# A two-layer graph network on one core: the first graph's transposes by halves, the last graph's last head by itself

## The chip, the cores and the metric

The kernel runs on one core of one Trainium2 chip. A core has a matrix engine (TensorE, in the profile PE, its weight loads PEld), a vector engine (VectorE, DVE), a scalar engine (ScalarE, ACT), GpSimd (POOL) and SyncE (SP), which here issues nearly all DMAs. Each engine works through its own list of instructions in order; semaphores hold an instruction back until its inputs are there. The metric is the time of one execution on the device, in microseconds (us); of several executions the median is given.

## The reference

Sixteen graphs, each with 1024 nodes of 256 features (`x`) and an adjacency matrix `adj` (int32; in these data 0 or 1, symmetric, ones on the diagonal). Two layers, each followed by a residual sum and a layer norm over the features (no gain, no offset):

```python
# layer 0: gate every edge by a sigmoid of a bilinear score, then sum over neighbours
e0    = leaky(einsum('bid,bjd->bij', x * a0[:, 0], x))        # slope 0.2
alpha = sigmoid(where(adj == 1, e0, -big))    # e1, e2, e3 for adj == 2, 3, 4
x     = layernorm(x + einsum('bij,bjd->bid', alpha, x) + bias)
# layer 1: graph attention, 4 heads of 64
Wh    = (x @ W).reshape(B, N, 4, 64)
e     = leaky_relu(e_src[:, :, None] + e_dst[:, None, :], 0.2) # Wh with a_src, a_dst
alpha = softmax(where(adj > 0, e, -1e9), axis=2)
x     = layernorm(x + elu(einsum('bijh,bjhf->bihf', alpha, Wh)).reshape(B, N, 256))
```

## The kernel before

All sixteen graphs go through a fast path that holds for adjacency of 0 and 1 and for scores of moderate size. While it runs it gathers three things that tell whether that held: sums of each adjacency matrix and its transpose (`sums`), the span of the attention scores (`span`), and the largest reciprocal of a softmax denominator (`zinv`). At the end they become one flag; it is loaded into a register of every engine (L1339), and a branch (L1342) leads to a general path that is not taken with these data.

**One graph.** Nodes stand in eight blocks of 128 (index `ib` or `jb`), in two halves of four. The function `stages` (from L197) makes a dictionary of Python generators, one for each kind of step; each `yield` ends one step.

- Loading: `xload` (L256, in two halves for the first graph, whole for the others), `aload` (L264, eight DMAs of 512 KB into two buffers), `cast` (L273, adjacency to bf16 on ACT, with its sum). The transposed adjacency comes from `turn`: in the first graph by PE (L283), in all others by a transposing DMA on SP's queue (L288). `mask` (L295, ACT) makes the 0/1 mask from it.
- Layer 0: `xt` transposes x on PE (L308), four blocks into one PSUM tile: for each of two feature blocks `c` and each half of the nodes; `xtc` copies the result to SBUF (L318; in the first graph on DVE, else on ACT). `xta` multiplies by a0 (L330 on DVE in the first graph, L332 on ACT in the others); `a_sb` holds a0 to a3, and a0 is loaded in `make_constants` (L65) by SP, after the two halves of x and two blocks of adjacency. `score` (L344, PE) needs both feature blocks of 512 nodes at a time. Then `leak` (L356, ACT), `leaky` (L364, DVE), `sigmoid` (L370, ACT), the transposes of the lower triangle (`below`, L383, PE, tile `pg`), masking (`lower` L389, `upper` L400, `self_loop` L407, DVE), `agg` (L415, PE), `residual` (L447), layer norm (`moments` L432, `gathered` L438, `spread` L456 and L457 on POOL, `shift` L465, `norm` L475 on DVE or L477 on ACT).
- Layer 1: transposes (`yt` L486), projection by W with the score vectors `wa` appended (`project` L505, `wh`), scores of sources (`sources` L523, `rows` L529, through DRAM at L541 and back as a broadcast, `sload` L636, tile `sbc`: one load for each half and head). The exponential of the leaky sum is split into products of factors, so that the softmax is a sum over edges with a positive score (`pos`, L646 on DVE, a comparison with the mask) and over all edges (`total`, L701 on PE, from `allm`, L693 on ACT). `acc` (L658, PE) sums `pos` against the factors `gm`, which are kept in a high and a low part (L621 ACT, L628 DVE). `acc_low` (L673, ACT) and `acc_sum` (L681, DVE) bring both parts together in `u`, for each half, head and pair of blocks.
- The end of a graph: `weigh` (L758, then a multiplication by `rho`), `divide` (L768, L771, L773, a multiplication by the reciprocal), `elu` (L793, ACT), `join` (L785, L787), layer norm, and the store (`leave`, L802 on SP; two stores for the second half of the last graph), which also updates `zinv` (L804). The multiplications (`times`) are one DVE operation for both blocks and all heads (L751); in the last two graphs they are eight small ACT operations instead (L746).

**Order.** `issue` (L1142) sorts all steps of all graphs by a time, and calls them in that order; the framework keeps the order as it is. The times only set the order. Three tables hold them: FIRST for the first graph, LAST for the last, TIMES for the fourteen between, which repeat with a period of 112. So the work of neighbouring graphs is interleaved: layer 0 of a graph beside layer 1 of the one before. Two `xload`s and two `aload`s precede all of it, then the constants. The checks that make the flag (L1316 to L1337) come after the whole planned list, outside it, and the framework's own scheduler places them: some DVE operations of them run ahead of the last `acc`, the rest after the last norm.

PSUM: four banks with the tag `pt` serve every transposed block, score, `agg`, `tot` and `pw`; two larger tiles serve `acc`. Four SBUF buffers with the tag `sbc` serve `vecs` (the score vectors), `wa`, the products and the broadcast rows.

Of the kernel before, what the change touches and what calls it, by code (L numbers as in the profile page):

```python
# [47 lines left out]
def make_constants(nc, k, const, work):  # L48
    D = k.D
    k.ident = const.tile([P, P], F32, name="ident")  # L50
    make_identity(nc, k.ident)
    k.ident16 = const.tile([P, P], BF16, name="ident16")
    make_identity(nc, k.ident16)
    k.mhalf = const.tile([P, 1], F32, name="mhalf")
    nc.gpsimd.memset(k.mhalf, -0.5)
    k.ones_r = const.tile([P, P], F32R, name="ones_r")
    ones = work.tile([P, P], F32, tag="ones", name="ones")
    nc.gpsimd.memset(ones, 1.0)
    nc.scalar.copy(k.ones_r, ones)
    k.ones = k.ones_r.bitcast(F32)  # L60
    k.a_sb = const.tile([P, k.DC, NK], F32, name="a_sb")
    k.w_aug = const.tile([P, k.DC, k.WD], F32, name="w_aug")
    k.bias_bc = const.tile([P, D], F32, name="bias_bc")
    a0 = k.inputs[0][0]
    nc.sync.dma_start(out=k.a_sb[:, :, 0:1], in_=a0.rearrange("(c p) o -> p c o", p=P))  # L65
# [131 lines left out]
def stages(nc, k, pl, b, xg, adjg, outg, sums, span, zinv):  # L197
# [104 lines left out]

    def xt():
        for c in range(DC):
            for half in range(NH):
                pt = t["xt", c, half] = quads("pt")
                for q in range(NQ):
                    nc.tensor.transpose(  # L308
                        pt[:, q, :], t["xb"][:, half * NQ + q, c * P : (c + 1) * P], k.ident
                    )  # L310
                yield

    def xtc():
        t["xT"] = pl.big.tile([P, DC, N], F32, tag="xT", name="xT")
        for c in range(DC):
            for half in range(NH):
                copy = nc.vector.tensor_copy if first else nc.scalar.copy
                copy(  # L318
                    t["xT"][:, c, half * HALF : (half + 1) * HALF],
                    t["xt", c, half].rearrange("p q n -> p (q n)"),  # L320
                )
                yield
# [391 lines left out]
    def parts(half, pair):  # L714

        u = t["u", half, pair]
        return u[..., 0:F], u[..., F : 2 * F], u[..., 2 * F], u[..., 2 * F + 1]

    def second(half, pair):

        return t["u", half, pair][..., F : 2 * F + 1]

# [18 lines left out]
    def times(val, by):  # L741

        if late:
            for q in range(2):
                for h in range(H):
# [7 lines left out]
    def weigh():  # L753
        for half, pair in PAIRS:
            ib = half * NQ + 2 * pair
            u2 = second(half, pair)
            if half:
                nc.vector.tensor_tensor(u2, t["ts", pair][..., 0 : F + 1], u2, ALU.subtract)  # L758
                yield
            times(u2, t["rho"][:, ib : ib + 2])  # L760
            yield

    def divide():
        t["rz"] = small("rzs", NB, H)
        for half, pair in PAIRS:
            ib = half * NQ + 2 * pair
            o, u2, z2, z1 = parts(half, pair)
            nc.vector.tensor_tensor(o, o, u2, ALU.add)  # L768
            yield
            rz = t["rz"][:, ib : ib + 2]  # L770
# [8 lines left out]
    def join():  # L779
        for half, pair in PAIRS:  # L780
            o, ex, _, _ = parts(half, pair)
            yp = t["y", half][:, 2 * pair : 2 * pair + 2, :].rearrange(
                "p q (h f) -> p q h f", h=H
            )
            nc.vector.scalar_tensor_tensor(o, o, 0.0, yp, ALU.max, ALU.add)  # L785
            yield
            nc.vector.scalar_tensor_tensor(yp, ex, 1.0, o, ALU.min, ALU.add)  # L787
            yield

    def elu():  # L790
        for half, pair in PAIRS:
            o, ex, _, _ = parts(half, pair)
            nc.scalar.activation(ex, o, AF.Exp)  # L793
            yield

    def leave():
        for half in range(NH):
# [5 lines left out]
            if half == NH - 1:  # L803
                nc.vector.tensor_tensor(zinv, zinv, t["rz"], ALU.max)  # L804
            yield

# [11 lines left out]
        weigh=weigh(), divide=divide(), elu=elu(), join=join(),  # L818
        moments1=moments("1"), gathered1=gathered("1"),
        spread1=spread("1"), shift1=shift("1"), norm1=norm("1"), leave=leave(),  # L820
    )

# [104 lines left out]
    "leave": [206.44, 240.93],  # L927
}
FIRST = {
    "aload": [-145.70, -145.40, -144.40, -143.60, -141.20, -140.10],  # L930
    "cast": [-146.10, -145.60, -144.60, -143.90, -142.60, -142.00, -140.90, -139.50],
    "turn": [-145.90, -145.10, -144.50, -143.20, -142.30, -141.30, -140.30, -139.30],
    "mask": [-145.30, -144.90, -143.80, -142.80, -141.70, -141.10, -139.40, -139.10],
    "setup": [-142.90, -140.70, -138.30],
    "xt": [-147.20, -147.10, -147.00, -146.80],
    "xtc": [-146.90, -146.70, -146.60, -146.40],
    "xta": [-146.50, -145.80, -144.20, -142.20, -141.80, -139.90, -139.60, -137.00],
    "score": [
        -146.20, -145.50, -144.80, -144.70, -143.40, -143.10, -142.10, -141.50, -140.40,
        -138.90, -138.60, -136.60,  # L940
    ],
    "leak": [
        -145.20, -144.30, -144.10, -144.00, -143.00, -142.70, -141.60, -141.40, -139.70,
        -138.50, -137.70, -136.40,
    ],
    "leaky": [
        -145.00, -143.70, -143.50, -143.30, -142.40, -141.90, -141.00, -140.60, -139.20,
        -137.90, -137.30, -135.60,
    ],
    "sigmoid": [-142.50, -140.80, -138.20, -137.10, -136.10, -135.00, -133.50, -132.80],  # L950
    "below": [
        -140.50, -140.20, -138.80, -138.00, -137.50, -136.80, -135.70, -135.20, -134.30,
        -132.70,
    ],
    "lower": [
        -140.00, -139.80, -138.40, -136.70, -136.00, -135.90, -134.90, -134.70, -133.40,
        -131.90,
    ],
    "upper": [-139.00, -137.60, -136.50, -135.10, -134.20, -133.00, -132.30, -131.80],
    "self_loop": [-138.70, -137.40, -135.50, -134.60, -133.80, -132.50, -131.60, -131.20],  # L960
    "agg": [
        -138.10, -137.80, -137.20, -136.20, -135.30, -134.80, -134.50, -133.90, -133.60,
        -133.20, -132.60, -132.40, -132.10, -131.40, -131.30, -130.60,
    ],
    "residual": [-136.90, -134.40, -133.70, -133.30, -133.10, -132.00, -130.90, -130.20],
    "moments0": [-135.80, -134.10, -132.90, -132.20, -131.10, -130.70, -130.40, -130.10],
    "gathered0": [-135.40, -134.00, -131.70, -131.50, -130.50, -130.30, -96.07, 17.17],
    "spread0": [-131.00, 20.28],
    "shift0": [-130.80, 24.26],
    "norm0": [6.67, 11.00, 11.41, 12.51, 25.36, 25.99, 26.71, 27.01],  # L970
    "yt": [17.15, 19.47, 29.04, 29.13],
    "ytc": [19.36, 19.69, 29.17, 29.53],
    "project": [20.27, 22.38, 25.24, 26.22, 32.78, 40.85, 41.12, 41.80],
    "wh": [25.15, 27.94, 28.22, 36.80, 41.06, 42.84, 42.85, 44.25],
    "sources": [43.57, 44.67],
    "rows": [44.50, 47.17],
    "keep_rows": [46.30, 54.62],
    "top_dve": [46.04, 47.34, 49.10, 49.48, 50.03],
    "top_pe": [46.11, 49.26],
    "exps": [51.13],  # L980
    "product": [51.24, 51.61, 51.65, 55.99, 64.09, 71.97, 73.66, 74.28],
    "high": [54.44, 56.34, 58.73, 61.00, 69.95, 72.79, 74.04, 74.66],
    "low": [54.68, 57.50, 65.30, 66.50, 71.75, 77.68, 77.72, 77.72],
    "sload": [50.22, 76.32, 79.88, 84.60, 99.79, 115.99, 126.87, 141.84],
    "pos": [
        56.38, 56.65, 59.61, 60.83, 61.90, 62.47, 66.98, 72.25, 78.79, 79.58, 80.30,
        81.29, 81.91, 83.89, 85.64, 86.24, 94.25, 94.83, 97.97, 99.15, 100.99, 101.36,
        101.95, 101.97, 105.63, 106.23, 106.73, 107.47, 108.82, 109.31, 109.42, 109.44,
        111.05, 111.90, 112.37, 114.78, 114.79, 114.81, 115.82, 117.22, 117.23, 120.53,
        122.14, 122.30, 123.00, 123.69, 124.94, 127.40, 128.22, 130.84, 132.75, 133.15,  # L990
        134.26, 137.15, 140.15, 141.06, 143.44, 144.05, 145.63, 146.94, 153.65, 154.27,
        155.46, 159.89,
    ],
    "acc": [
        61.10, 61.65, 61.72, 63.59, 69.81, 72.90, 74.47, 75.10, 81.40, 83.30, 83.92,
        84.50, 84.62, 86.15, 88.72, 89.34, 98.53, 98.69, 100.90, 100.97, 102.11, 102.79,
        105.80, 106.18, 108.03, 108.18, 108.25, 109.02, 109.72, 109.72, 110.35, 110.44,
        113.56, 114.38, 116.31, 117.04, 117.43, 119.10, 119.20, 119.89, 122.26, 122.73,
        122.79, 124.03, 124.41, 124.82, 125.15, 127.73, 134.85, 139.77, 140.29, 142.76,
        143.64, 145.00, 145.14, 146.56, 153.78, 155.85, 158.96, 159.35, 164.01, 166.21,  # L1000
        166.25, 166.99,
    ],
    "acc_low": [
        76.14, 76.54, 89.55, 94.31, 106.18, 107.05, 110.80, 113.01, 119.96, 120.50,
        133.26, 133.40, 149.44, 150.74, 167.23, 167.69,
    ],
    "acc_sum": [
        78.38, 79.46, 93.10, 94.97, 106.56, 107.30, 111.03, 113.02, 120.66, 120.80,
        133.29, 134.06, 151.18, 151.58, 167.52, 167.84,
    ],  # L1010
    "all_edges": [
        -136.30, 12.13, 78.67, 81.11, 84.67, 85.86, 89.41, 101.01, 104.36, 105.17, 108.79,
# [375 lines left out]
```

## Time and profile before

| what | us |
|---|---|
| three runs | 1746.99, 1749.58, 1750.99 |
| median | 1749.58 |
| profiled execution, own time | 1748.92 |
| its span | 1747.1 |
| first score matmul starts | 9.62 |
| last `acc` ends, about | 1724.5 |
| last `bn_aggr` ends | 1737.64 |
| last norm ends | 1740.39 |
| flag made | 1741.66 |

The span runs from the first to the last instruction that the profiler shows; the execution's own time is 1.8 us longer. The page of the profile gives busy shares of each engine, the span in 40 slices (a digit is tenths of busy time), the chain of work that ended last, groups of instructions by line, and DMAs. A timeline line gives start, duration, engine, line, operation, output <- inputs, shapes, count of like instructions in a row, and in brackets how long the engine had been idle and what released it. DVEq, SPq and the like are the engines' sequencers.

### The profile page before, as it was taken

Reading aid. Unit: us, or ns where it says so; the run is one execution under the profiler, and the core shown is the slowest. Engines: PE = TensorE matmul, PEld = TensorE weight load, DVE = VectorE, ACT = ScalarE, POOL = GpSimd, SP = SyncE. Lnnn points to the kernel's source line nnn. Section 1 sums busy time; section 2 is a strip of 40 time slices with the busy share of each in tenths; the row PEclk is TensorE's granted clock in tenths of the full one; section 3 lists DMA queues with packets and bytes.
Section 4 is the critical chain, followed back from the end, with each engine's and each line's share of the span. In section 5 each row is a group of like instructions: output and inputs, shape, how many; then the busy total and the mean of one; then the engine's idle time right before and its main releaser. Section 6 shows DMA issues by size and latency. Waiting matters only on the chain.

```text
span 1747.1 us, 29629 instructions
## 1 busy us (share of the span) xinstructions
PE 1695.6 (97%) x10579; PEld 1494.8 (86%) x10579; DVE 1639.0 (94%) x3640; ACT 1237.6 (71%) x2770; POOL 107.1 (6%) x138
## 2 busy tenths in 40 slices
PE   7999999999999999999999999999999999999884
PEld 4789898998979889898998989889898998979883
DVE  4498999999999999999999999999999999999997
ACT  6673967759587685967759586685957769585675
POOL 0001000010000101000010000101000010000100
PEclk9999999999999999999999999999999999999987
DMA  5452343434334343343434334343342435331020
GB/s 184 109 127 75 93 109 88 109 91 129 90 90 101 109 119 91 98 98 91 109 93 135 81 98 108 99 115 91 97 110 78 109 74 139 79 74 49 26 67 26
DMA packets 249274, 168.60 MB, mean 97 GB/s; under 512 B 133280, under 2 KB 232736, under 8 KB 249120
## 3 DMA queue, kind: packets, MB, share of 16 engines
q1 hardware_dynamic: 249120, 166.63, 36.3%
q8 instruction: 86, 1.41, 0.3%
q14 instruction: 68, 0.56, 0.1%
HBM read 118.10 MB, written 17.04 MB: 77 GB/s over the span
## 4 chain that ended last, share of the span: by engine, by line
PE 83%; issue 7%; DVE 4%; ACT 3%; DMA 1%; POOL 0%; SPq 0%; POOLq 0%; ACTq 0%; DVEq 0%
PE agg L415 24%; PE acc L658 24%; PE tot L701 13%; PE e L344 11%; PE pw L505 6%; PE pg L383 2%; DVE pos L646 1%; PE pt L308 1%; PE pt L486 1%; DMA sbc<-sdram 1%; DMA aT<-a 0%; ACT mT L295 0%; ACT a L273 0%; DVE gm L628 0%; DVE gate L364 0%
## 5 line engine op out<-in xcount | busy, mean ns | idle before, releaser
L646 DVE SCALAR_TENSOR_TENSOR pos<-sbc,nd,mT 128x512 fp32r<-128x512 f32 x1024 | 732.0, 738 | 7.6 <-DMA sbc<-sdram 4.5
L658 PE MATMUL acc<-gm,pos 128*128 128x260 f32 x4096 | 613.3, 293 | 6.5 <-DVE u L681 2.8
L658 PEld LDWEIGHTS acc<-gm,pos 128*128 128x128 f32 x4096 | 538.7, 190 | 19.5 <-issue 3.8
L415 PE MATMUL agg<-xb,gate 128*128 128x256 f32 x2048 | 463.3, 379 | 0.0
L415 PEld LDWEIGHTS agg<-xb,gate 128*128 128x128 f32 x2048 | 380.0, 190 | 46.9 <-DVE gate L407 0.6
L701 PE MATMUL tot<-gm,allm 128*128 128x264 f32 x2048 | 328.4, 297 | 7.1 <-ACT gm L621 5.0
L701 PEld LDWEIGHTS tot<-gm,allm 128*128 128x128 f32 x2048 | 281.1, 190 | 11.7 <-ACT gm L621 5.2
L344 PE MATMUL e<-xT,xTa 128*128 128x512 f32 (+3 forms) x768 | 265.6, 490 | 3.1 <-ACT xTa L332 1.6
L344 PEld LDWEIGHTS e<-xT,xTa 128*128 128x128 f32 x768 | 135.3, 191 | 106.9 <-issue 53.4
L673 ACT COPY low<-acc 128x260 f32<-128x260 f32 x256 | 89.9, 377 | 190.3 <-PE acc L658 190.3
L693 ACT CAST allm<-mT 128x512 fp32r<-128x512 uint8 x256 | 157.5, 616 | 27.9 <-PE tot L701 26.6
L477 ACT ACTIVATE y<-y,shift,rstd 128x256 f32<-128x256 f32 x254 | 136.8, 591 | 41.8 <-DVE shift L465 41.8
L273 ACT ACTIVATE a<-a 128x1024 bf16<-128x1024 int32 x128 | 135.6, 1060 | 41.0 <-DMA aT<-a 19.3
L295 ACT ACTIVATE mT<-aT 128x1024 uint8<-128x1024 bf16 x120 | 127.2, 1060 | 6.4 <-DMA aT<-a 6.3
L456 POOL TENSOR_SCALAR std<-mv 128x4 f32<-128x4 f32 x64 | 27.0, 421 | 1626.0 <-DVE mv L438 1426.5
L364 DVE TENSOR_TENSOR gate<-e,gate 128x512 f32<-128x512 f32 x192 | 104.2, 550 | 21.3 <-ACT gate L356 21.2
L505 PE MATMUL pw<-w_aug,yT 128*128 128x264 f32 x512 | 122.2, 387 | 0.7 <-ACT yT L495 0.6
L681 DVE TENSOR_TENSOR u<-acc,low 128x260 f32<-128x260 f32 x256 | 102.1, 419 | 16.6 <-ACT low L673 16.6
L432 DVE BATCH_NORM_STATS2 st<-y 128x6 f32<-128x256 f32 x256 | 105.8, 415 | 1.2
L505 PEld LDWEIGHTS pw<-w_aug,yT 128*128 128x128 f32 x512 | 93.4, 190 | 15.6 <-ACT yT L495 1.7
L356 ACT ACTIVATE gate<-e 128x512 f32<-128x512 f32 x192 | 90.0, 486 | 14.6 <-PE e L344 14.5
L400 DVE TENSOR_TENSOR gate<-gate,mT 128x1024 f32<-128x1024 f32 (+7 forms) x128 | 95.8, 748 | 4.5 <-PE pg L383 2.4
(97 smaller groups left out, 1775.9 us busy)
## 6 DMA issues: line engine op xcount, KB each, us to landing
a<-in_adj_dram SPq DMA_DIRECT2D x128, 512.0 KB, 4.7
sbc<-sdram SPq DMA_DIRECT2D x128, 256.0 KB, 4.6
out_dram<-y SPq DMA_DIRECT2D x31, 512.0 KB, 3.5
xb<-in_x_dram SPq DMA_DIRECT2D x15, 1024.0 KB, 5.2
aT<-a SPq DMA_TRANSPOSE x120, 3.1
xb<-in_x_dram SPq DMA_DIRECT2D x2, 512.0 KB, 4.2
sdram<-srow SPq DMA_DIRECT2D x32, 8.0 KB, 1.4
out_dram<-y SPq DMA_DIRECT2D x2, 256.0 KB, 2.3
```

The source lines that it names most:

```text
L273: nc.scalar.activation(t["a16", ib], t["a32", ib], AF.Copy, accum_out=sums[:, 0, at : at + 1])
L295: nc.scalar.activation(t["mT"][:, :, ib * P : (ib + 1) * P], t["aT", ib], AF.Square, accum_out=sums[:, 1, at : at + 1],)
L344: nc.tensor.matmul(e[:, 0:n], lhsT=t["xTa", jb][:, c, :], rhs=t["xT"][:, c, at : at + n], start=(c == 0), stop=(c == DC - 1),)
L364: nc.vector.tensor_tensor(ge, t["e", jb, at][:, 0:n], ge, ALU.max)
L415: nc.tensor.matmul(agg[:, 0:D], lhsT=t["gate"][:, jb, ib * P : (ib + 1) * P], rhs=t["xb"][:, jb, :], start=(jb == 0), stop=(jb == NB - 1),)
L432: nc.vector.bn_stats(st, t["y", half][:, q, :])
L477: nc.scalar.activation(y, y, AF.Identity, bias=shift, scale=rstd)
L505: nc.tensor.matmul(pw[:, 0:WD], lhsT=t["yT"][:, c, jb * P : (jb + 1) * P], rhs=k.w_aug[:, c, :], start=(c == 0), stop=(c == DC - 1),)
L646: nc.vector.scalar_tensor_tensor(p_, t["sbc", half, h], t["nd"][:, jb, h : h + 1], t["mT"][:, jb, half * HALF : (half + 1) * HALF], ALU.is ...
L658: nc.tensor.matmul(t["acc", half, h, q // 2][:, q % 2, 0 : 2 * E], lhsT=t["pos", half, h, jb][:, q * P : (q + 1) * P], rhs=pl.gm[:, h, jb] ...
L693: nc.scalar.copy(m_, t["mT"][:, j0 : j0 + 4, ib * P : (ib + 1) * P])
L701: nc.tensor.matmul(tot[:, 0 : H * F1], lhsT=t["allm", ib, jb // 4 * 4][:, jb % 4, :], rhs=pl.gm[:, :, jb, l, F:E], start=(jb == 0 and l == 0),
```

## The change

1. `a_sb` is allocated, and a0's DMA issued, ahead of the loads of x and adjacency; the DMA is ScalarE's instead of SP's.
2. In the first graph the transposes of x go by halves: both feature blocks of the first half, then both of the second. Of their copies, those of feature block 0 stay on DVE, those of feature block 1 go to ACT.
3. In the last graph's second half, heads 0 to 2 go through `weigh`, `divide`, `elu` and `join` without head 3, which has generators of its own: `weigh_end`, `divide_end`, `elu_end`, `join_end`. Its multiplications are on DVE instead of ACT. The joins of heads 0 to 2 are split by blocks (two instructions instead of one each). In other graphs the new generators only yield.
4. The checks become a generator, `verdict`, and take places in the planned order; the flag is now made ahead of the last norm. Every graph's update of `zinv` moves from `leave` to `verdict`.
5. FIRST and LAST have new times throughout. TIMES keeps all its values and gains those of the new generators.

In the instruction lists of both programs, PE's middle (items 861 to 7994 of 9869 compiled ones) and ACT's 1783 middle instructions stand in the same order; DVE's differ there only in the place of `zinv`. On SP, `vecs` and W are issued after adjacency block 3 of the first graph instead of block 5, and in the last graph the loads of `sbc` stand between single transposes (transpose, `aload`, `sbc`, transpose, `sbc`, transpose, `sbc`), where before two transposes stood ahead of two of them.

```diff
-    k.a_sb = const.tile([P, k.DC, NK], F32, name="a_sb")
-    a0 = k.inputs[0][0]
-    nc.sync.dma_start(out=k.a_sb[:, :, 0:1], in_=a0.rearrange("(c p) o -> p c o", p=P))
...
+        k.a_sb = const.tile([P, k.DC, NK], F32, name="a_sb")
+        nc.scalar.dma_start(out=k.a_sb[:, :, 0:1], in_=a0.rearrange("(c p) o -> p c o", p=P))
         for name in ("xload", "aload", "aload"):
             next(graphs[0][name])
...
+    PARTS = [(c, half) for c in range(DC) for half in range(NH)]
+    if first:
+        PARTS.sort(key=lambda part: part[1])
     def xt():
+        for c, half in PARTS:
...
     def xtc():
+        for c, half in PARTS:
+            copy = nc.vector.tensor_copy if first and c == 0 else nc.scalar.copy
...
+    def heads(half):
+        return slice(0, H - 1 if last and half else H)
...
     def weigh():
         for half, pair in PAIRS:
+            ib, hs = half * NQ + 2 * pair, heads(half)
+            u2 = second(half, pair)[:, :, hs]
             if half:
+                ts = t["ts", pair][:, :, hs, 0 : F + 1]
+                nc.vector.tensor_tensor(u2, ts, u2, ALU.subtract)
                 yield
+            times(u2, t["rho"][:, ib : ib + 2, hs])
...
     def join():
+            rows = (0, 1) if last and half else (slice(0, 2),)
+            for q in rows:
+                nc.vector.scalar_tensor_tensor(o[:, q], o[:, q], 0.0, yp[:, q], ALU.max, ALU.add)
...
+    END = [(H - 1, pair) for pair in range(NQ // 2)]
+    def divide_end():
+        for h, pair in END:
...
+            nc.vector.tensor_tensor(z2, z2, rho, ALU.mult)
+            for q in range(2):
+                nc.vector.scalar_tensor_tensor(
+                    o[:, q], u2[:, q], rho[:, q : q + 1], o[:, q], ALU.mult, ALU.add
+                )
+            yield
+            nc.vector.scalar_tensor_tensor(rz, z1, Z_MIN, z2, ALU.max, ALU.add)
+            yield
+            nc.vector.reciprocal(rz, rz)
+            yield
+            for q in range(2):
+                nc.vector.tensor_scalar(o[:, q], o[:, q], rz[:, q : q + 1], None, ALU.mult)
+            yield
...
     def leave():
-            if half == NH - 1:
-                nc.vector.tensor_tensor(zinv, zinv, t["rz"], ALU.max)
...
+    def verdict():
+        if last:
...
+            nc.vector.tensor_reduce(more, sums, AX.X, ALU.add)
+            nc.vector.tensor_tensor(more[:, 0:1], more[:, 1:2], more[:, 0:1], ALU.subtract)
+            nc.vector.tensor_scalar(span[:, 1], span[:, 1], -1.0, None, ALU.mult)
+            nc.vector.tensor_reduce(
+                worst[:, 1:2], span.rearrange("p s b h -> p (s b h)"), AX.X, ALU.max
+            )
+        yield
...
+        nc.vector.tensor_tensor(zinv, zinv, t["rz"], ALU.max)
+        yield
...
+            nc.vector.tensor_scalar(k.flag, good, 0.0, None, ALU.is_equal)
+        yield
```

## The prediction

> **What bounds the kernel now.** I read the page first: busy shares, slices, the chain that ended last.
>
> ```profile
> PE 1695.6 (97%) x10579; PEld 1494.8 (86%) x10579; DVE 1639.0 (94%) x3640; ACT 1237.6 (71%) x2770; POOL 107.1 (6%) x138
> PE   7999999999999999999999999999999999999884
> DVE  4498999999999999999999999999999999999997
> PE 83%; issue 7%; DVE 4%; ACT 3%; DMA 1%; POOL 0%; SPq 0%; POOLq 0%; ACTq 0%; DVEq 0%
> ```
>
> PE is full from slice 2 to slice 37; only the first slice and the last three (43.7 us each) have room. DVE, at 9 in between, is a near second. The change alters the order of the first graph, the last graph and their neighbours; the order of the middle is the same. So I read the ends by windows (columns: length, then busy time and count of PE, PEld, DVE, ACT, POOL, then clock, DMA share, GB/s).
>
> ```profile
> 0.00:10.00 10.00, 4.29 (x17) 3.55 (x18) 3.10 (x8) 2.62 (x4) 1.26 (x10) 1.00 0.66 216
> 10.00:20.00 10.00, 10.00 (x39) 5.03 (x39) 2.22 (x7) 5.69 (x12) 0.00 (x0) 1.00 0.29 100
> 20.00:30.00 10.00, 7.31 (x47) 4.32 (x45) 3.16 (x9) 9.97 (x18) 0.00 (x0) 1.00 0.66 213
> 30.00:40.00 10.00, 8.18 (x46) 5.41 (x45) 8.92 (x21) 8.97 (x18) 0.00 (x0) 1.00 0.82 273
> 1640.00:1660.00 20.00, 15.63 (x100) 13.93 (x99) 18.13 (x48) 14.44 (x47) 1.30 (x3) 0.91 0.06 16
> 1700.00:1724.50 24.50, 21.15 (x147) 19.55 (x145) 23.02 (x45) 11.26 (x41) 0.00 (x0) 0.93 0.00 1
> 1724.50:1737.70 13.20, 0.14 (x2) 0.00 (x0) 11.41 (x32) 12.16 (x41) 1.60 (x2) 0.63 0.00 0
> ```
>
> Until 10 us the kernel waits for data, then PE is the slow one, from 20 to 30 ACT (9.97 of 10), and from about 40 PE. From 1640 on DVE leads (18.13 of 20, 23.02 of 24.5), and after the last `acc`, at 1724.5, DVE and ACT hand work to and fro. Lastly the timeline of the head, and of the two places where the end waits.
>
> ```profile
> 4.41 1.09 PE L308 MATMUL pt<-ident,xb 128*128 128x128 f32 x4 [4.41 <-DMA xb<-in_x_dram]
> 6.22 2.82 PE L308 MATMUL pt<-ident,xb 128*128 128x128 f32 x12 [0.72 <-DMA xb<-in_x_dram]
> 9.19 0.48 DVE L330 TENSOR_SCALAR xTa<-xT,a_sb 128x128 f32<-128x128 f32 x2 [0.27 <-DMA a_sb<-in_L_gnn_a_dram]
> 9.62 3.75 PE L344 MATMUL e<-xT,xTa 128*128 128x512 f32 x4 [0.58 <-DVE xTa L330]
> 14.31 1.06 ACT L273 ACTIVATE a<-a 128x1024 bf16<-128x1024 int32 x1 [5.36 <-PE pa L283]
> ```
>
> ```profile
> 1556.95 11.35 SPq L288 DMA_TRANSPOSE aT<-a  x2
> 1573.24 0.75 DVE L646 SCALAR_TENSOR_TENSOR pos<-sbc,nd,mT 128x512 fp32r<-128x512 f32 x1 [2.05 <-DMA sbc<-sdram]
> ```
>
> ```profile
> 1739.30 1.09 ACT L477 ACTIVATE y<-y,shift,rstd 128x256 f32<-128x256 f32 x2 [2.16 <-DVE shift L465]
> 1741.52 0.14 DVE L1337 TENSOR_SCALAR flag<-good 1x1 int32<-1x1 f32 x1
> ```
>
> The first score matmul, at 9.62, waits for `xTa`, and that for a0 (issued 2.81, landed 6.3 later). In the tail the flag, done at 1741.66, is the last thing before a fixed 5.44 us of register loads and branches.
>
> **Head.** Before, the transposes go c0h0, c0h1 (waits for the second half of x), c1h0, c1h1; the first score needs c0h0 and c1h0. After, both first-half ones come first: four at the old pace, 4.41 to 5.50, four more to about 6.4, then the second half to 8.2. The copy of c1h0 goes to ACT: 0.56 (a 128x512 copy at L318 later on) from about 6.5. DVE copies c0h1 at 7.3 to 8.0, as the planned order has it before `xTa`, then `xTa` takes 0.48 from 8.03, and the first `e` starts at about 8.55 instead of 9.62: **1.07 us earlier**. This needs a0 by 8.0; issued at about 0.7 and at the 3.6 to 4.0 that the later loads into a_sb took (6.3 at most), it lands between 4.3 and 7.0. SP, relieved of 0.43 of issue, gains nothing: its next load waits for a buffer. `vecs` and W are issued after adjacency load 3 instead of 5; `wa` (eight DVE ops, 3.2 us) moves from 30.8 to about 24, where DVE has 3.16 of 10 busy. Were that cover gone, `xTa` behind it would cost up to 3.2.
>
> On ACT two copies (1.1) now stand before cast 0, which moves from 7.61 to about 8.85. That is hidden: its transposes follow the first `e`, at about 12. Cast 1 goes from 14.31 to 13.15, and the ACT-bound stretch follows 0.9 to 1.0 earlier in my replay (each instruction started when its inputs and engine are free, with durations from rows). By 38 us, 0.65 of `pg` work on PE is done that was not done before. From there PE is full, so the lead stays: **-1.2**. Bounds: +1.0 (a0's small pieces hold up x by as much as the 6.3 landing exceeds 3.6, less the gain) and -3.0 (PE at its later pace from the start: the four `e` took 3.75 against 1.98 at 20.26, so -1.8 more). I take the replay.
>
> The pace first: the first four `e` took 3.75 and eight turns 1.06; later the same took 1.98 and 0.61, although the clock column says 1.00 in all three windows. [...]
>
> The a0 row (6.3 us behind 2 MB of x and adjacency, against 3.6 to 4.0) says place matters. [...]
>
> **Last graph up to the last `acc`.** The 2.05 wait of DVE at 1573 (and 1.05 of PE behind it) exists because SP issued two transposes, which held its queue 11.35, ahead of `sbc`. In the new order each load of `sbc` stands behind a single one. Gain 1.05 to 2.05 if none of them waits long. Six small check operations (0.9) leave the stretch before 1724.5, where DVE leads: up to -0.9. Against it: the tables are new for the whole graph, so waits move. PE waits for `src` on ACT 2.6 and for `gm` on DVE 1.7 around 1655; in the new order the `src` of the second half comes behind 28 more `acc`, which hides some of that, while aggregation is spread later. Nearest rows for what a reordered wait is worth: 0.95 to 2.6 either way. I take **-1.5**, with -3.5 and +2 as ends.
>
> **After the last `acc`.** The last head by itself adds 20 DVE operations (subtract, four of divide's with two by rows, join; both pairs). Neighbouring rows have 0.17 (8 wide) to 0.28 (128 wide); at 0.2: +4.0. The other heads' four wide operations per pair (2.77 together) shrink to three quarters: -1.4. Joins by rows add four instructions at 0.14 (what 0.28 for 128 and 0.69 for 512 columns leave at zero columns): +0.6. Checks ahead of the norm: +0.9. Sum +4.1 of DVE work. Against that stand DVE's idle 1.8 in this window, a good 1.5 that can run before the last `acc`, since heads 0 to 2 no longer wait for head 3, and eight fewer small ACT operations of 0.25. So the last `bn_aggr` moves from 1737.6 to 1738.4, the norm's end from 1740.4 to 1741.1, and SP has issued the last store at 1741.6. The flag, ready by 1737.5, no longer adds its 1.27 us behind the norm (1740.39 to 1741.66). Those cancel: **-0.1**; ends -1.5 (the branches of the engines that wait early overlap) and +3.0 (none of the 4.1 hidden, less 1.27).
>
> **Sum.** -1.2 -1.5 -0.1 = -2.8 from the profiled execution's 1748.92: **1746.1**. That execution is 0.66 below the median of 1749.58, so against the median it is -3.5, or 0.2%: exactly where a measurement of this kernel begins to tell a difference from none.
>
> **Rivals.**
> A: PE gets its later pace during the transposes (-1.8), and the tail gives what the flag cost (-1.2): 1743.1. [...] Against it: ACT is full from 20 to 30, so an earlier PE must also find its adjacency rows loaded.
> B: the gains are hidden: a0 or the loads of adjacency still set the head, and waits in the last graph only move. Tail and head cancel: about 1748.6. For it: adjacency load 2 goes out when cast 0 frees its buffer at about 9.9 and takes 4.7 to land, so cast 2 can't come before 14.6, and DVE is over 90% busy in the last 100 us.
> C, slower: SP's queue at the start of the last graph. Three loads of `sbc` now each stand behind one transpose, which waits for its cast on ACT. A load feeds eight `pos` (8 x 0.74 = 5.9) and takes 4.6 to land, so from about 1.3 us of holding on each wait counts. At the 2.05 of the one wait in the trace, three cost 6.15, and the -1.5 doesn't come: 1748.92 - 1.2 - 0.1 + 6.15 = 1753.8. For it: two transposes held the queue 11.35. Against it: ACT is not full there.
>
> **How the numbers follow.** Forecast 0.45 (1744 to 1748; half of it below the bound of 1746.1), A 0.22, B 0.20, C 0.13. Faster by over 0.2%: 0.23 + 0.22 = 0.45; within: 0.22 + 0.20 = 0.42; slower: 0.13. The range is 1741 to 1752: it takes in A with its head at -3, B, and the ends of the last graph and the tail taken singly (+2, +3), and leaves out C.
>
> **What would show it.** Head: first `e` at 8.5, cast 1 at 13.2, PE full by 39 with the first graph's last `agg` 1.2 earlier. A0 landing after 8 or an `xTa` waiting for `a_sb` would refute it; so would `e` x4 near 2 us (A). Last graph: no DVE wait for `sbc` over 1 us; if there are three, it is C. Tail: last `acc` about 2.7 earlier than 1724.5, the span's end 22.5 after it, the flag before the last norm, DVE nearly gapless in between. Most likely wrong: the reordered last graph, whose replay is the loosest.

## The result and the profile after

Over 15 runs each the kernel before has a median of 1749.29 us (1746.8 to 1753.2) and the changed one 1744.86 (1744.0 to 1748.0). The medians are 4.4 us apart. The ratio of all runs is 0.9977, with a 95% interval of 0.9970 to 0.9983: 0.23% or 4.0 us faster. (Here and below the ratio lies near that of the means, so it can differ a little from the quotient of the medians.) The forecast was 1746.1 in a range of 1741 to 1752. The profiled execution took 1745.48, its span is 1743.5, against 1747.1 before.

The page of the changed kernel, in the lines that answer to those of before (busy times, slices of PE and DVE):

```profile
PE 1693.9 (97%) x10579; PEld 1494.5 (86%) x10579; DVE 1638.4 (94%) x3662; ACT 1240.4 (71%) x2768; POOL 106.5 (6%) x138
PE   7999999999999999999999999999999999999884
DVE  5498999999999999999999999999999999999997
```

The slices tell nothing at this size, and the chain of this page holds only the last norm, so that it says nothing on the middle. Windows of the changed kernel (length, then busy time and count of PE, PEld, DVE, ACT, POOL, then clock, DMA share, GB/s):

```profile
0.00:10.00 10.00, 3.73 (x17) 3.39 (x17) 2.01 (x7) 2.43 (x4) 1.26 (x10) 1.00 0.64 210
10.00:20.00 10.00, 9.91 (x43) 5.11 (x44) 3.50 (x10) 8.53 (x18) 0.00 (x0) 1.00 0.61 184
20.00:30.00 10.00, 7.31 (x45) 4.20 (x44) 5.97 (x15) 9.97 (x18) 0.00 (x0) 1.00 0.53 182
30.00:40.00 10.00, 8.90 (x56) 6.41 (x55) 7.46 (x17) 7.79 (x17) 0.00 (x0) 1.00 0.69 227
1721.00:1735.20 14.20, 1.02 (x4) 0.58 (x3) 13.76 (x69) 10.37 (x35) 1.42 (x2) 0.62 0.00 0
```

In the first 10 us PE does less than before (3.73 against 4.29), from 10 to 20 us ACT does half as much again (8.53 against 5.69), and after the last `acc` DVE is nearly gapless: 69 operations, 13.76 of 14.2. The timeline of the changed head shows what happened there:

```profile
6.05 3.65 PE L309 MATMUL pt<-ident,xb 128*128 128x128 f32 x16 [6.05 <-DMA xb<-in_x_dram]
9.49 0.87 DVE L330 TENSOR_SCALAR xTa<-xT,a_sb 128x128 f32<-128x128 f32 x4
9.91 2.38 PE L344 MATMUL e<-xT,xTa 128*128 128x512 f32 x4 [0.22 <-DVE xTa L330]
12.13 0.61 PE L280 MATMUL pa<-ident,a 128*128 128x128 bf16 x8
12.83 1.06 ACT L270 ACTIVATE a<-a 128x1024 bf16<-128x1024 int32 x1 [1.47 <-issue]
```

x comes 1.64 later than before (6.05 against 4.41), so the first score starts 0.29 **later**, at 9.91. But the sixteen transposes now run without a gap, the four scores take 2.38 instead of 3.75 and the eight turns 0.61 instead of 1.06, and cast 1 starts at 12.83 instead of 14.31. The last steps of the changed kernel:

```profile
1734.13 0.14 DVE L908 TENSOR_SCALAR flag<-good 1x1 int32<-1x1 f32 x1
1735.31 3.20 SPq L864 DMA_DIRECT2D out_dram<-y  x3
1736.82 1.09 ACT L477 ACTIVATE y<-y,shift,rstd 128x256 f32<-128x256 f32 x2 [1.54 <-DVE shift L465]
```

The flag is ready 3.6 ahead of the end of the last norm (1737.91); the span ends 5.6 after that norm (6.7 before).

**Where the time went.** To compare executions I cut each span at three events that all kernels have: the start of the 17th residual of layer 0 (the first of the third graph), that of the 120th (the last of the fifteenth graph), and the end of the last `acc`. "Full pace" is the instant at which the trace's clock record begins; ahead of it matmuls took about twice as long (the first four scores 3.75 ahead of it in before, 1.95 behind it in before_again; eight turns 1.06 and 0.61). All times in us. Four kernels without a median here were run once, for the profile.

| kernel | full pace | to 17th | to 120th | to last acc | to end | span | median |
|---|---|---|---|---|---|---|---|
| before | 14.47 | 235.52 | 1295.31 | 193.81 | 22.41 | 1747.05 | 1749.29 |
| before_again | 8.29 | 233.34 | 1296.07 | 193.52 | 22.84 | 1745.76 | |
| after | 10.78 | 232.97 | 1296.06 | 192.02 | 22.46 | 1743.52 | 1744.86 |
| head_only | 9.96 | 232.22 | 1297.24 | 193.93 | 22.66 | 1746.05 | 1748.53 |
| last_only | 14.14 | 235.79 | 1297.88 | 191.26 | 22.36 | 1747.29 | 1747.81 |
| a0_old | 13.30 | 233.97 | 1297.61 | 191.87 | 22.56 | 1746.02 | 1746.49 |
| a0_mid | 9.53 | 231.45 | 1297.09 | 191.53 | 22.38 | 1742.45 | 1744.84 |
| sbc_swap | 13.78 | 235.57 | 1296.35 | 191.77 | 22.44 | 1746.13 | |
| swap_timed | 9.37 | 234.26 | 1296.47 | 192.06 | 22.72 | 1745.52 | 1748.22 |
| tail_joined | 10.95 | 233.15 | 1297.29 | 191.46 | 22.88 | 1744.77 | |
| verdict_late | 9.21 | 233.96 | 1296.56 | 192.15 | 23.47 | 1746.14 | |
| before_warm | 4.79 | 233.49 | 1297.45 | 193.87 | 22.55 | 1747.36 | 1749.28 |
| mid_warm | 9.28 | 231.36 | 1296.20 | 191.83 | 22.38 | 1741.77 | 1744.91 |

Between the two profiles of the result: head -2.55, middle +0.75, last graph -1.79, tail +0.05; together -3.5. (swap_warm's profiled execution, 5 above its own median, is told of with its run; it is left out of the ranges of the stretches below.)

### The profile page after: what moved, and what is told of

Same layout as the page of the kernel before. It is cut to its first block, busy times and chain, and to the rows that moved or that the text cites. A ratio compares the mean times of both kernels' runs of the same rounds, so it can differ in the third digit from the quotient of the medians.

```text
span 1743.5 us, 29658 instructions
## 1 busy us (share of the span) xinstructions
PE 1693.9 (97%) x10579; PEld 1494.5 (86%) x10579; DVE 1638.4 (94%) x3662; ACT 1240.4 (71%) x2768; POOL 106.5 (6%) x138
## 5 line engine op out<-in xcount | busy, mean ns | idle before, releaser
L364 DVE TENSOR_TENSOR gate<-e,gate 128x512 f32<-128x512 f32 x192 | 104.3, 550 | 14.5 <-ACT gate L356 14.4
```

The source lines that it names most:

```text
L364: nc.vector.tensor_tensor(ge, t["e", jb, at][:, 0:n], ge, ALU.max)
```

## The experiments

**Head alone and last graph alone.** head_only is the kernel before with the first diff below and the changed FIRST; last_only is the changed kernel with those taken back.

```diff
-    nc.sync.dma_start(out=k.a_sb[:, :, 0:1], ...)          # behind the first loads
+        nc.scalar.dma_start(out=k.a_sb[:, :, 0:1], ...)    # ahead of them
-        for c in range(DC):
-            for half in range(NH):
+        for c, half in PARTS:                              # by halves; copies of c = 1 on ACT
```

> The kernel before with the head of the change alone: a0 first through ScalarE's queue, transposes and copies by halves, the first graph's new times; last graph and checks as before. My theory: the head is worth about half of the 4.4 us, as the lead in the trace of the changed kernel is 2.7 when the orders of both kernels meet again (270 us), and 1.7 later on: 1746.6 to 1747.6, last acc to end as before (22.6). It should show x landing near 5.9 again and not 4.3, since a0's small pieces travel beside it. Rival: the head is worth nothing by itself, because the lead is used up by the steady middle (1749), and all of the gain is the last graph's.

Measured: 1748.53, ratio 0.9990 (0.9981 to 0.9998). By the median that is 0.8 below before (1749.32 beside it), less than expected and nearer to the rival's 1749; by the ratio it is 1.7, as expected. The first stretch took 232.22, the last two 193.93 and 22.66. x landed at 5.66.

> The changed kernel with the head of before (a0 on SyncE's queue behind the first loads, transposes in the old order, four copies on VectorE, the first graph's old times); the last graph with its separate head, new times and planned checks is kept. My theory: 1.7 to 2.2 less than before (1747.1 to 1747.6), all of it ahead of the last acc, none behind it: last acc to end 22.4 to 22.7. x lands at 4.3 again and the first score starts near 9.6. Rival: the separate head and the planned checks shorten the tail by over 1, and then last acc to end is under 21.6.

Measured: 1747.81, ratio 0.9991 (0.9982 to 1.0000). That is just above what I expected. The gain of its last graph is ahead of the last `acc` (191.26 against 193.81), none behind it (22.36). The rival of a shorter tail falls. Each part shows its own stretch shortened and the other as before, so the parts don't hang together. The two medians add up to 2.3 below before, not 4.4; the two ratios add up to 0.19% of the 0.23%. With 1.5 of uncertainty each neither is a contradiction, but the stretches are the better measure.

**a0's place.** a0_old puts its load on SyncE's queue again, behind x and two blocks of adjacency; a0_mid on the same queue between them:

```diff
-        nc.scalar.dma_start(out=k.a_sb[:, :, 0:1], in_=a0.rearrange("(c p) o -> p c o", p=P))
         for name in ("xload", "aload", "aload"):
             next(graphs[0][name])
+            if name == "xload":      # a0_mid; in a0_old after the loop
+                nc.sync.dma_start(out=k.a_sb[:, :, 0:1], in_=...)
```

> The changed kernel, with a0 again on SyncE's queue behind the two halves of x and two blocks of adjacency; all else changed. My theory: x lands at 4.3 instead of 5.9, since nothing small travels beside it, and a0 at about 9, so that the first score starts at about 9.6 to 9.9, as in the changed kernel: within 0.7 of its 1744.9. Rival: a0's place is what the head gains by; then it loses about 1.5 and stands at 1746.4 or above.

Measured: 1746.49, ratio 0.9980 (0.9971 to 0.9989). By the medians it is 1.6 above the changed kernel, which is the rival's figure; by the ratios (0.9980 against 0.9977) only 0.5, which is mine. The intervals overlap, so the times don't decide between the two. x landed at 4.49, but `xTa` waited for a0 until 9.34, PE had a gap of 1.60 ahead of the first score (9.88), and full pace came at 13.30.

> The changed kernel, with a0 on SyncE's queue between the two halves of x and the adjacency. My theory: the first half of x lands at 4.3, its second half by about 1 later than 6.2 at most, a0 by 7, so the first score starts at about 8.5 and the head gains up to 1.3 on the changed kernel: 1743.6 to 1744.9. Rival: x at 5.9 in the changed kernel is chance and not a0's doing; then x lands between 4.3 and 5.9 here too, and the time is the changed kernel's.

Measured: 1744.84, ratio 0.9972 (0.9961 to 0.9983), the changed kernel's time. Its head is nevertheless what was expected: x landed at 4.54 (4.57 in mid_warm), as in all kernels with a0 behind x (4.27 to 4.86), while all four profiles with a0 first had it at 5.64 to 5.92. The two groups don't overlap, so x's later landing was no chance.

```profile
4.67 3.65 PE L309 MATMUL pt<-ident,xb 128*128 128x128 f32 x16 [4.67 <-DMA xb<-in_x_dram]
8.54 2.45 PE L344 MATMUL e<-xT,xTa 128*128 128x512 f32 x4 [0.21 <-DVE xTa L330]
11.52 1.06 ACT L270 ACTIVATE a<-a 128x1024 bf16<-128x1024 int32 x1 [1.53 <-PE pa L280]
```

Score and cast 1 come 1.3 to 1.4 earlier than in the changed kernel, and the first stretch is 1.5 shorter (231.45 against 232.97). The medians don't show that 1.5, and the ratios (0.9972 against 0.9977) only 0.9 of it: it is near what such a comparison can tell, and the middle in the table differs by up to 2.6 between executions.

**A second look at before, and one swapped pair.** sbc_swap changes a single number in LAST of the kernel before, so that SP issues transpose, `sbc`, transpose, `sbc`:

```diff
-    "turn": [..., -41.19, -35.31, -25.39],
+    "turn": [..., -41.19, -32.70, -25.39],
```

> The kernel before, unchanged, for a second profile. In the first profile the stretch from the 17th residual of layer 0 (235.5) to the 120th (1530.8) took 1295.3; in five kernels with the same order there it took 1296.1 to 1297.9. My theory: that is chance, not the change, so a second look gives 1296 to 1298 here, with 235.3 to 236.0 ahead of it, 193.6 to 194.1 from there to the last acc, and 22.4 to 22.7 behind that. Rival: something in the change makes the middle longer; then it is 1295.3 again, within 0.3.

Measured: the middle took 1296.07, as the theory had it, and 193.52 and 22.84 after it. The surprise is the head: 233.34 instead of 235.52, with the same instructions. PE's timeline of the second profile of before:

```profile
4.81 1.09 PE L308 MATMUL pt<-ident,xb 128*128 128x128 f32 x4 [4.81 <-DMA xb<-in_x_dram]
6.19 2.53 PE L308 MATMUL pt<-ident,xb 128*128 128x128 f32 x12 [0.29 <-DMA xb<-in_x_dram]
9.61 1.95 PE L344 MATMUL e<-xT,xTa 128*128 128x512 f32 x4 [0.89 <-DVE xTa L330]
11.40 0.61 PE L283 MATMUL pa<-ident,a 128*128 128x128 bf16 x8
```

The first score starts at the same 9.61, but takes 1.95 instead of 3.75: full pace came at 8.29 instead of 14.47. The four scores are 1.80 shorter for it and the eight turns behind them 0.45 (0.61 instead of 1.06), together the 2.2 by which the first stretch differs.

> The kernel before with one number changed: in the last graph's times the seventh transpose goes behind the load of the row sbc that it stood ahead of, so that SyncE issues transpose, sbc, transpose, sbc instead of two transposes and two sbc. My theory: the wait of 2.05 for sbc at the 1573rd us on VectorE goes, and with it 1.05 on TensorE; from the 120th residual to the last acc 191.8 to 192.9 instead of 193.8 (the changed kernel has 192.0, and 191.3 to 191.9 in its variants), so the swap alone gives at least half of what the last graph gained. Rival: the wait only moves to another step, and the stretch stays at 193.5 to 194; then the gain is the other new times'.

Measured: 191.77, all that the last graph's change gives (191.3 to 192.2 in the kernels with it, 193.5 to 193.9 without). The time was saved where the wait had been. Windows from 1560 to 1600, first of before, then of sbc_swap:

```profile
1560.00:1600.00 40.00, 38.72 (x260) 35.20 (x259) 37.29 (x74) 27.37 (x61) 0.00 (x0) 1.00 0.32 70
1560.00:1600.00 40.00, 39.89 (x268) 36.59 (x267) 38.59 (x77) 27.87 (x61) 0.00 (x0) 1.00 0.34 75
```

In these 40 us PE stands idle for 1.3 to 2.2 in the four profiles without the swap, and for 0.2 at most in the nine with it. The clock is not the cause: half pace (0.5 in the clock record) takes 17.07 of the stretch up to the last `acc` in before and 20.48 in sbc_swap and in the changed kernel.

DVE's waits over 0.5 from 1560 to 1660 in this kernel:

```profile
DVE span L548 <- ACT wh L517: 1.2, 1, 1.2
DVE gate L400 <- ACT mT L295: 1.1, 1, 1.1
DVE y L447 <- DMA out_dram<-y: 1.0, 1, 1.0
DVE gm L628 <- ACT gm L621: 0.6, 1, 0.6
```

The wait of 2.05 for `sbc` is gone; part of it comes back as 1.1 for `mT` and 1.0 (0.6 before) for a store's buffer, at places where PE is not held up. SP's queue shows the swap:

```profile
1557.59 1.23 SPq L288 DMA_TRANSPOSE aT<-a  x1
1565.40 0.38 SPq L636 DMA_DIRECT2D sbc<-sdram  x1
1567.68 1.23 SPq L288 DMA_TRANSPOSE aT<-a  x1
1568.96 0.57 SPq L636 DMA_DIRECT2D sbc<-sdram  x1
```

The first `sbc` goes out at 1565.40, 3.0 earlier than in the first profile of before, although this kernel runs 1.1 behind that profile at the 120th residual.

> The kernel before with the one swapped transpose and sbc load again, now timed. My theory: the profile's 2.0 between the 120th residual and the last acc is in the time too: median 1746.8 to 1748.2, against 1749.3 before and 1747.8 for the whole of the last graph's change. Rival: the new times, the separate head and the planned checks are needed for the last graph's gain: 1748.8 or above.

Measured: 1748.22, ratio 0.9993 (0.9984 to 1.0002): 1.4 below before, in the direction expected, and at its upper end; the interval does not exclude no change. The stretch took 192.06 again.

**The tail in two parts.** tail_joined lets head 3 go with the others (and its first subtraction comes behind the last head's sum); verdict_late plans the last four steps of the checks behind the last norm.

```diff
-        return slice(0, H - 1 if last and half else H)
+        return slice(0, H)                       # tail_joined; the four *_end only yield
-    "verdict": [5941.96, 5975.61, 6027.35, 6055.62, 6085.49, 6138.78, 6170.81],
+    "verdict": [5941.96, 5975.61, 6027.35, 7100.0, 7110.0, 7120.0, 7130.0],   # verdict_late
```

> The changed kernel, but the last graph's last head goes with the other three again (multiplications on ScalarE, joins unsplit), and its first subtraction comes after the last head's sum; checks planned as changed. My theory: the separate head gives no more than its extra instructions cost; last acc to last bn_aggr 13.5 to 14.2 (13.0 before, and 0.9 of checks), to the end 22.0 to 22.7, as with it (22.46). Rival: the separate head is what lets the planned checks in; without it the end comes 23.3 or more after the last acc.

Measured: the last `bn_aggr` ends 13.66 after the last `acc` (14.09 with the separate head), the span 22.88 after it. The end is 0.2 beyond what I expected and 0.4 short of the rival. The separate head costs 0.4 ahead of the norm; the span of this execution ends 6.46 behind the norm, where the other kernels with an early flag have 5.5 to 5.7. So much the end varies without a reason that I found.

> The changed kernel with the last four steps of the checks (zinv, its maximum and the limits, the transpose, the flag) planned behind the last norm, as they ran before; the separate head stays. My theory: the last bn_aggr comes 13.2 to 13.6 after the last acc (14.1 with the checks ahead), the flag 1.3 behind the norm, and the end 9.4 to 9.7 behind bn_aggr (8.4 with the flag early, 9.4 before): 22.6 to 23.2 in all, against 22.46. Rival: the end hangs on the stores, not on the flag; then it stays 8.4 behind bn_aggr, and 21.6 to 22.0 in all.

Measured: 13.25 to the last `bn_aggr`, 10.22 from there, 23.47 in all; the last two lie above what I expected. The theory holds in sign: the early flag is worth 1.9 behind `bn_aggr` (1.2 if the late flag is taken at 9.6, the mean of the six kernels of the table with the old tail) and costs 0.84 ahead of it. The tail of verdict_late:

```profile
1737.59 1.09 ACT L477 ACTIVATE y<-y,shift,rstd 128x256 f32<-128x256 f32 x2 [1.30 <-DVE shift L465]
1738.24 0.19 DVE L889 TENSOR_TENSOR zinv<-zinv,rzs 128x32 f32<-128x32 f32 x1
1739.81 0.14 DVE L908 TENSOR_SCALAR flag<-good 1x1 int32<-1x1 f32 x1
```

Flag at 1739.95, 1.27 behind the norm, and the end 6.2 later.

**The pace by itself.** Idle transposes of the identity run on PE from 1.46 on, ahead of x; nothing reads their bank. before_warm adds twelve to the kernel before (to 4.28), swap_warm twelve to sbc_swap, mid_warm ten to a0_mid (to 3.86).

```diff
         pl.fill()
+        warm = pl.ps_t.tile([P, 4, P], F32, tag="pt", name="warm")
+        for i in range(12):
+            nc.tensor.transpose(warm[:, i % 4, :], k.ident, k.ident)
```

> The kernel before with twelve idle transposes of the identity on TensorE ahead of those of x, from about 1.9 us on, in a PSUM bank that nothing reads; all else as before. Ten profiles so far show TensorE at half pace until the end of a first stretch of 3.41 us in which it was busy for 0.91 or more of the time; stretches of 0.84 or less didn't do. My theory: the early transposes leave no gap up to the first score, so full pace is recorded by 9 us (14.5, 14.1, 13.8 and once 8.3 in kernels with this head), the first score still starts at 9.4 to 10.0, and up to the 17th residual it takes 233.0 to 233.8 (235.5 with late full pace, 233.3 with early). Median 1 to 2 below before: 1747.3 to 1748.5. Rival: the pace is not what makes the head shorter, but the order of its steps: 235.3 to 235.8, median 1749.3.

Measured: the profiled execution does what the theory says (full pace at 4.79, scores in 1.95, 233.49), but the median is 1749.28, ratio 0.9999 (0.9990 to 1.0008). For the time the rival's figure is right.

> The kernel before with two small edits: the swapped transpose and sbc load of the last graph, and the twelve idle transposes at the start; no new tables, a0 where it was, checks behind the end, heads together. My theory: the two account for nearly all of the change: 233.0 to 233.8 up to the 17th residual, 191.6 to 192.2 from the 120th to the last acc, 22.4 to 22.8 behind it, median 1744.8 to 1746.5. Rival: the rest of the change (order of halves, new times, separate head, planned checks) is needed for at least half of the gain: 1747 or above.

Measured: 1747.98, ratio 0.9990 (0.9981 to 0.9999): the rival's side, and about the swap's own 1.4. In the profiled execution, 1753.05, the idle transposes did not bring an early pace: full pace came only at 13.91, and twice, at 31.0 and 85.6, half pace came back for 3.41.

```profile
1.46 2.82 PE L1315 MATMUL warm<-ident 128*128 128x128 f32 x12 [1.46 <-POOL ident masks.py:199]
4.68 1.11 PE L308 MATMUL pt<-ident,xb 128*128 128x128 f32 x4 [0.40 <-DMA xb<-in_x_dram]
6.13 2.82 PE L308 MATMUL pt<-ident,xb 128*128 128x128 f32 x12 [0.34 <-DMA xb<-in_x_dram]
9.50 3.75 PE L344 MATMUL e<-xT,xTa 128*128 128x512 f32 x4 [0.55 <-DVE xTa L330]
```

PE still has gaps of 0.40, 0.34 and 0.55, and in the three stretches of 3.41 ahead of 10.50 it was busy for 0.65, 0.78 and 0.84 (more on such stretches below).

> The changed kernel with a0 on SyncE's queue between x and the adjacency, and ten idle transposes ahead of those of x. My theory: full pace by 8 us, first score at 8.0 to 8.6, up to the 17th residual 230.2 to 231.3 (231.45 with full pace at 9.5; 233.0 in the changed kernel), median 0.5 to 2 below the changed kernel: 1743.0 to 1744.4. Rival: the adjacency's loads and ScalarE bound the head from here on: 231.3 to 231.7, and 1744.8.

Measured: 1744.91, ratio 0.9974 (0.9963 to 0.9984); first score at 8.50, full pace at 9.28, 231.36. The rival's figures came, and nothing is gained on a0_mid. But full pace came only 0.25 earlier than there, so that whether a pace by 8 us would have helped was not put to the test. No version beat the changed kernel by more than these comparisons can tell.

## Why the prediction came out: its steps one by one

**Head, -1.2: right in sign, short in size (-2.55 between the two profiles), and wrong in the step.** I had the first score 1.07 earlier. It is 0.29 later. The failed step is "four at the old pace, 4.41 to 5.50": x did not land at its old time. I named the effect, as the end of +1.0, and took zero; it is 1.64 between the two profiles, 1.2 in the mean of all. With it the first score gains nothing: 9.63 to 9.91 with a0 first, 9.37 to 10.06 in the old order without idle transposes. a0's 256 pieces of four bytes went through their queue from 2.86 to 5.33, and in that time the DMA records show x moving 80 to 105 KB in each half us, against 140 to 195 before. a0 itself landed where I had it (5.64, expected 4.3 to 7.0). Where x did land at its old time, the step came true: in a0_mid the first score starts at 8.54, against 8.55 in my replay.

What made up for it between these two profiles is what I had put into rival A: the pace. A's -1.8 was an estimate from the two durations of the four scores (3.75 and 1.98); what brings the pace was not shown then. In the fourteen profiles full pace began at the end of a stretch of 3.41 us, on a grid of such stretches whose place differed from run to run (the later changes in each trace's clock record lie whole multiples of 3.41 behind its first: 481 to 502 of them in before and in the changed kernel). In these profiles a stretch in which PE was busy for a share of 0.88 or more brought it each time (1.00 in before, 0.94 in the changed kernel); of eight between 0.73 and 0.84, one did (0.83, in swap_timed). With the gaps of the first profile of before (0.72 and 0.58), no stretch ahead of the first score is full enough wherever the grid lies, and an estimate that slides the grid over its timeline (bound 0.86, between the 0.84 and the 0.88 above) puts full pace at 12.6 to 16.0; with the smaller first gap of its second profile, at 8.0 to 16.0; with the gapless transposes of the changed kernel, at 9.0 to 12.4. The recorded instants are 14.5, 14.1, 13.8, 9.4 and 8.3 with the old head, 9.2 to 11.0 with the new one and a0 first. So with the old head the pace came early in some profiled executions and late in others, and the first profile of before had it late: the -2.55 is in part luck. The mean first stretch of the four profiles with the changed head and a0 first (233.1) is 1.8 below that of the five with the old head and no idle transposes (234.9).

The order by halves helps by leaving no gap (the sixteen transposes ran on for 3.65; before had 0.72 of idle time ahead of its last twelve), and also by what comes first. At early full pace the old head takes 233.3 (before_again; 233.5 in before_warm), the new one 232.2 to 233.2 with a0 first: 0.2 to 1.1 below before_again. With x at its old time it takes 231.4 and 231.5 (mid_warm, a0_mid), 1.9 below before_again; that is nearer to what my replay was about, and a0's place cost most of it. (Two profiles with early pace, swap_timed and verdict_late, are left out here because half pace came back at 81 us.) With late full pace the old head takes 235.5 to 235.8 (13.8 to 14.5), the new one 234.0 (13.3, a0_old). These are single executions, and the medians of before_warm speak against making more of the pace: how often before runs with early pace is not known from its times, and the share of the pace in the 4.4 stays open.

A stretch did not have to be wholly busy to bring full pace: 0.88 sufficed. Half pace returned once or twice in three of the fourteen profiles (verdict_late, swap_timed, swap_warm) after stretches with PE busy for 0.49 to 0.56, while others of 0.49 to 0.62 passed without, which I can't explain.

That a0's place matters was right, and the trace gives the price: while the small pieces went through another queue, the large load beside them moved at about half its rate (80 to 105 KB in each half us against 140 to 195). No run sends a0 as one piece, or first on SyncE's own queue, so that the part of the pieces and the part of the other queue are not told apart.

**Last graph, -1.5: right, -1.8, by the step named.** One swapped pair on SP gives -1.75 to -2.0 by itself against the first profile of before (-1.5 to -2.2 against the four without it), and PE's idle time at the old wait is gone with it. The two other ends did not matter: the 0.9 of checks that left the stretch shortened nothing that can be seen, and the other new times gave nothing beyond the swap. In the medians alone the swap is not clear of noise (swap_timed). Rival C did not come: no wait for `sbc` is listed on DVE from 1560 to 1660 in the changed kernel.

**Tail, -0.1: right.** +0.05 between the two profiles; means of 22.60 over the six profiles of the table with the old tail and 22.43 over the five with the new one. The step behind it was right too: I had `bn_aggr` later by 0.75 (1.09) and the flag's wait of 1.27 gone. One reading was wrong: the 5.44 from the flag to the end is not fixed. With a late flag it is 5.4 to 5.8 in seven profiles and 6.2 in verdict_late. The two planned parts pull against each other, the separate head costing 0.4 and the early flag netting 0.4 to 1.0.

**Middle, nothing: right.** It differs between executions by 1295.3 to 1297.9 with unchanged order, so that single spans can't be compared to better than about 2.

**Sum.** -2.8 from the profiled execution was forecast, -3.4 came between the two (1748.92 to 1745.48), -4.4 between the medians. The total came out partly because two errors in the head cancelled: x 1.6 later, PE at its later pace 3.7 earlier. The second of these was in part the late pace of the one execution that I compared with. Rival B (gains hidden) falls with the two shorter stretches (by the means of the profiles -1.8 and -2.0); of rival A the pace came, the gain in the tail did not.

## What to carry to other kernels

Cut the spans of several executions at events that they share before explaining a difference of two or three us: here one stretch of unchanged work varied by 2.6, and the same head by 2.2. SP's queue, held for 11.35 by two transposes ahead of `sbc`, was worth reading instruction by instruction: one load moved ahead of a blocked transpose gave in its stretch what a whole table of new times gave (191.77 in sbc_swap and 192.06 in swap_timed, against 192.02 in the changed kernel). A tiny load in many pieces, started beside the load that everything waited for, put that one off by some 1.2 here; right behind it, it was still in time (first score at 8.54 in a0_mid).

## What the runs showed of the hardware that was not expected

- 256 pieces of 4 bytes took 4.9 us to land on an otherwise empty queue (the changed kernel), and x on the other queue landed some 1.2 later for it (mean of four profiles 5.75, 5.64 to 5.92, against 4.27 to 4.86 in the others).
- The clock column reads 1.00 from the start, but matmuls ran at about half pace until the trace's clock record began; only their durations show it (3.75 in before and 1.95 in before_again for the same four scores).
- Half pace returned for one stretch of 3.41 us early in the program in three of fourteen profiles (at 81 us in two, at 31 and 86 in swap_warm).
- From the last norm to the end of the span the same code took 5.5 to 5.7 and once 6.5 with the flag early.
